# Loading and unpacking the FP4 down weights of a decoder's last feed-forward by another queue and at another stage

## The chip, the cores and the metric

The kernel runs on one core of a Trainium2 chip. A core has five engines, each with its own instruction queue that it works through in order: TensorE (PE, matmuls; PEld is its loading of weights), VectorE (DVE), ScalarE (ACT), GpSimd (POOL) and SyncE (SP, which here only issues transfers). Transfers (DMA) can be issued from SP, ACT or POOL; they run beside the engines, and an instruction that needs the data waits for the landing. The metric is the device time of one execution in microseconds (us).

## The reference

A decoder of two layers with a layer norm after each sublayer, on x of 4 batches x 512 tokens x 512 features, in float32:

```python
x = _layernorm(x + _L0_attn_ref(x, ...))                       # phase A
x = _layernorm(x + _L0_xattn_ref(x, ctx_2048, ctx_2048, ...))  # phase B
x = _layernorm(x + _L0_ffn_ref(x, ...))                        # phase C
x = _layernorm(x + _L1_attn_ref(x, ...))                       # phase D
x = _layernorm(x + _L1_xattn_ref(x, ctx_2048, mask))           # phase E
x = _layernorm(x + _L1_ffn_ref(x, ...))                        # phase F
```

Two phases matter here. E is a cross attention of one head over `ctx` (512 rows of 512) with a mask: scores x·ctx / sqrt(512), softmax, and the readout of the same ctx rows. F is a gated feed-forward with weights packed in FP4, eight codes to a 32-bit word, and one float16 scale for each group of 128 inputs:

```python
w_gu = _dequant_fp4(gate_up_packed, gate_up_scales, 128)   # 2 x 1408 outputs, 512 inputs
w_down = _dequant_fp4(down_packed, down_scales, 128)       # 512 outputs, 1408 inputs
gate, up = split(x @ w_gu.T)
y = (silu(gate) * up) @ w_down.T
return y / sqrt(mean(y * y) + 1e-6)
```

## The kernel before

**Arithmetic.** Tiles are 128 partitions x 512. Where float32 accuracy is wanted, a value is held as a pair of float32r tiles, a rounded high part and the remainder. `split` (L135) makes the pair: the high part by a copy on ACT (L144, "CAST" in the profile), the low part as source minus high part by a tensor_tensor (L147), on DVE or, if asked for, on POOL. `split` also notes the last low part that was given to POOL in `self.low[True]`. A product of two pairs is three matmuls (L155 to L157).

**Order of the work.** Each phase is a Python generator for one batch: A0 to A3, B0, and so on to F3. `lanes` (L1307) steps two of them in turn, so that the end of one batch lies beside the start of the next; background generators prepare weights. `BESIDE` (L40) lists them as (first, last, key): such a generator makes one step per round while the last task started is one from `first` to `last`. `("E2", "E2", "F")` says: step `l1_ffn_weights` from the start of E2 to the start of E3. `need(key, ready)` (L1300) steps a generator on the spot until `ready()` holds. Within a generator, `Pipe.later(n, f)` calls `f` after n calls of `tick`. From the instructions that come of this, a scheduler of the tile framework makes the final order on each engine, and gives out buffers from pools of fixed size (69 "o", 13 "t", 12 "x", 4 "w" buffers in SBUF; 8 banks of PSUM). `issue_after(ins)` keeps an instruction behind `ins` in that order.

**Cross attention (E, `l1_xattn`, L1068).** For each batch: load x and the mask (mk); load ctx transposed (tiles ecT) and make pairs (ecTh on ACT, ecTl on POOL); transpose x on PE (ex) and make pairs (exh on ACT, exl on DVE); load ctx (ecn) and make pairs (ecnh on ACT, ecnl on POOL); scores es on PE; minimum and mask on DVE (ee, L1094); exponential on ACT (L1095); transpose (ep) and make pairs; readout pv on PE; add to x on DVE (L427); statistics (L212, L213); normalize (L236); store by SP (L239). All its loads go by SP's queue.

**Feed-forward (F, `l1_ffn`, L1172).** For each of 11 groups i of 128 inner features, the gate (u = 0) and up (u = 1) products each take four PSUM tiles fg (L1238), which are scaled and summed by ACT (L1186, L1190), DVE (L1194) and POOL (L1198); then silu on ACT (L1202), the product on DVE (L1206), a pair (L1211 on ACT, L1212 on POOL), and the down product facc on PE (L1221) with the pair `self.dn[i]`.

**F's weights.** `l1_ffn_codes` (L1108, key "F0", beside D) turns the gate and up codes into float values and stores them in a scratch in HBM, gu_codes. `l1_ffn_weights` (L1145, key "F") then loads, for each i, the two gate/up tiles from that scratch, the down scales (p4s) and the packed down codes (tile "p4" of the "w" pool, `p<-in_dn_p` in the profile), all by SP; `F_LOAD` = 5 ticks later, `down` unpacks: a shift and a mask on DVE (L1127, L1128), a multiplication by the scales on DVE (L1154), a high part on ACT (L144) and a low part on POOL (L147). The same operations are run eleven times, once for each i. L1232 makes F0 pull that generator until `self.dn` holds the next i.

In the profiled execution, two of the bit operations of each of the first four down loads stand in D, at 1056.9 to 1065.6 us; the multiplications and pairs start at 1156.2 (first multiplication) and 1202.3 (first high part), and end at 1318.4 (last low part), in F0.

Of the kernel before, what the change touches and what calls it, by code (L numbers as in the profile page):

```python
# [12 lines left out]
F16 = mybir.dt.float16  # L13
BF16 = mybir.dt.bfloat16
I32 = mybir.dt.int32
# [6 lines left out]
B, S, D = 4, 512, 512  # L22
P = 128
# [8 lines left out]
LOG_EXP = "natural_log_exp_and_others"  # L32
D_NEXT = 7
B_NEXT = 13
F_LOAD = 5
CODES_EVERY = 3
F_SCALED, F_ACT, F_PAIR, F_DOWN = 1, 5, 3, 9
ORDER = "A0 A1 A2 A3 B0 B1 B2 B3 C0 C1 C2 C3 D0 D1 D2 D3 E0 E1 E2 E3 F0 F1 F2 F3"

BESIDE = [("A1", "A3", "C0"), ("A3", "B0", ("B", 0)), ("B0", "B2", "C"), ("C3", "D0", "D"), ("D1", "D3", "F0"), ("E2", "E2", "F")]  # L40


class Pipe:
# [25 lines left out]
class Net:  # L69
# [1076 lines left out]
    def l1_ffn_weights(self):  # L1146

        yield from self.bg["F0"]
        nc, a, bits = self.nc, self.a, self.bits
        pipe = Pipe()  # L1150

        def down(w, sc):
            f = bits(w)
            nc.vector.scalar_tensor_tensor(f, f, 2.0 ** 126, sc, ALU.mult, ALU.mult)  # L1154
            self.dn.append(self.split(f, "p4", lo_eng=nc.gpsimd))

        for i in range(11):
            for u in range(2):
                pipe.tick()
                self.gu[i, u] = self.o("gu", F32R)  # L1160
                self.load(self.gu[i, u].bitcast(F32), self.gu_codes[i * 2 + u])
                yield
            pipe.tick()
            sc = self.load(self.t("p4s", F16), a["dn_s"][i : i + 1, :].to_broadcast([P, 512]))
            pipe.later(F_LOAD, down, self.load(self.w("p4", I32), a["dn_p"][i]), sc)
            yield
        yield from pipe.drain()

    def l1_ffn(self, b):
        nc = self.nc  # L1170
        pipe = Pipe()
# [57 lines left out]
            acc[t] = f  # L1229

        for i in range(11):
            self.need("F", lambda: len(self.dn) > min(10, i + 1))  # L1232
            for u in range(2):
                for g in range(4):
                    pipe.tick()
                    ps = self.pa("fg")
                    for n in range(2):
                        nc.tensor.matmul(ps, self.gu[i, u][:, g * P : (g + 1) * P], xT[g][n], start=n == 0, stop=n == 1)  # L1238
                    pipe.later(F_SCALED, scaled, i, u, g, ps)
                    yield  # L1240
# [93 lines left out]
def body(tc, args, phases=range(6)):  # L1334
    with ExitStack() as ctx:
# [9 lines left out]
        def step(n):  # L1345
            if len(phases) == 6:
                for first, last, key in BESIDE:
                    if plain.index(first) < n <= plain.index(last) + 1:
# [74 lines left out]
```

## Time and profile before

| what | value |
|---|---|
| median of 3 runs | 1580.09 us (1579.72 to 1582.03) |
| the profiled execution | 1580.57 us |
| its span, first to last instruction | 1578.9 us |
| granted TensorE clock | 0.994 |
| instructions | 25669 |
| gate and up products of F1 and F2 start at | 1338.2 and 1412.0 us |
| 128x512 matmul, start to start, in full flow | 0.2268 us |
| multiplication by the scales, L1154 (min / median / max of 11) | 658 / 689 / 1640 ns |
| shift L1127, mask L1128 (medians of all 33) | 542, 485 ns |
| high part of a p4 tile on ACT (median of 11) | 620 ns |
| low part of a p4 tile on POOL (median of 11) | 1292 ns |

How to read it: a group of instructions is named by its line, engine and operation, then output<-inputs, the tile forms and the count; busy time is the time in which an engine ran instructions. In a timeline, a line begins with its start and its length in us, and joins neighbours of one kind (x4); "[7.39 <-ACT exh L144]" at its end says that the engine had been idle for 7.39 us and that the end of ACT's exh released it. In the list of transfers, the last two columns are KB of one and the median us from issue to landing. Matmuls overlap in the pipeline, so a single one shows 0.39 us while one starts each 0.2268.

### The profile page before, as it was taken

The numbers are of one execution on the slowest core, as the hardware profiler recorded it, in microseconds if no ns is written. First come the engines' busy times: TensorE is split into PE (matmuls) and PEld (weight loads), VectorE is DVE, ScalarE is ACT, GpSimd is POOL, SyncE is SP. The second block draws the span as 40 slices with busy tenths as digits, with TensorE's granted clock in tenths as the row PEclk, the third lists the DMA queues.
The fourth block names the chain that finished last, engine by engine and source line by source line (L and its number), as shares of the span: only waits on it lengthen the run. The fifth ranks groups of instructions, "written<-read, shape, count | busy, mean of one in ns | idle before, by whom it ended". The sixth has DMA issues, their size and how long they took to land.

```text
span 1578.9 us, 25669 instructions
## 1 busy us (share of the span) xinstructions
PE 1512.4 (96%) x8222; PEld 1090.9 (69%) x8222; DVE 1214.0 (77%) x2594; ACT 1041.7 (66%) x2240; POOL 687.8 (44%) x704
## 2 busy tenths in 40 slices
PE   8999998999999999999999999999999999999996
PEld 6888775555544764477777668777687677787885
DVE  6486688898876678777577797767886898888896
ACT  5334667888778877887696864969634445545554
POOL 6665783656535303430435323353324344344342
PEclk9999999999999999999999999999999999999998
DMA  7044874444224534753434345633336630020101
GB/s 256 29 160 140 266 235 151 156 165 139 71 74 126 189 132 131 208 180 130 134 101 120 103 140 148 173 96 91 130 119 220 233 113 12 20 81 1 54 1 54
DMA packets 138759, 200.72 MB, mean 127 GB/s; under 512 B 17776, under 2 KB 52592, under 8 KB 138624
## 3 DMA queue, kind: packets, MB, share of 16 engines
q1 hardware_dynamic: 127584, 178.03, 35.5%
q10 hardware_dynamic: 6912, 12.59, 2.8%
q0 software_dynamic: 4128, 8.46, 2.2%
q8 instruction: 65, 1.06, 0.3%
q14 instruction: 70, 0.57, 0.1%
HBM read 121.94 MB, written 51.90 MB: 110 GB/s over the span
## 4 chain that ended last, share of the span: by engine, by line
PE 50%; DVE 11%; ACT 9%; issue 6%; DMA 3%; POOL 2%; SPq 0%; ACTq 0%; DVEq 0%; POOLq 0%
PE fg L1238 7%; PE facc L1221 5%; DVE fg L1194 3%; PE dT L986 3%; PE dn L794 2%; PE bo L500 2%; PE pg L740 2%; ACT de L976 2%; PE pu L742 2%; PE do L1006 2%; PE bT L249 2%; PE had L808 2%; PE bs L528 2%; PE ds L961 2%; PE dq L155 1%
## 5 line engine op out<-in xcount | busy, mean ns | idle before, releaser
L1194 DVE SCALAR_TENSOR_TENSOR fg<-fg,gs,fg 128x512 f32<-128x512 f32 x220 | 163.1, 745 | 30.4 <-ACT fg L1186 15.6
L976 ACT ACTIVATE de<-de,dm 128x128 f32<-128x128 f32 (+3 forms) x256 | 142.8, 562 | 11.5 <-DVE dm L972 11.3
L1238 PE MATMUL fg<-fxh,gu 128*128 128x512 f32 x352 | 140.4, 399 | 6.2 <-DVE fg L1194 3.1
L972 DVE CUSTOM_DVE_ANT_0 de<-ds,negm,thr 128x128 f32<-128x128 f32 (+3 forms) x256 | 126.3, 546 | 18.4 <-PE ds L961 15.8
L1238 PE MATMUL fg<-fxl,gu 128*128 128x512 f32 x352 | 137.5, 391 | 0.1
L717 POOL TENSOR_TENSOR hl<-g,hh 128x512 fp32r<-128x512 f32 x64 | 83.2, 1307 | 110.8 <-ACT hh L716 90.7
L484 POOL TENSOR_SCALAR be<-be,bsm 128x512 f32<-128x512 f32 x128 | 93.4, 742 | 85.3 <-DVE bsm L482 53.7
L1198 POOL TENSOR_TENSOR fg<-fg,fg 128x512 f32<-128x512 f32 x44 | 60.1, 1367 | 140.3 <-DVE fg L1194 56.7
L478 ACT ACTIVATE be<-bs,bsm 128x512 f32<-128x512 f32 x128 | 87.3, 689 | 32.4 <-DVE bsm L476 31.0
L898 POOL TENSOR_TENSOR dql<-dqf,dqh 128x512 fp32r<-128x512 f32 x32 | 41.4, 1295 | 150.6 <-ACT dqh L897 150.5
L986 PE MATMUL dT<-ident,de 128*128 128x128 f32 x640 | 91.3, 278 | 8.4 <-ACT de L976 6.4
L986 PEld LDWEIGHTS dT<-ident,de 128*128 128x128 f32 x640 | 71.7, 141 | 27.5 <-ACT de L976 14.8
L1238 PEld LDWEIGHTS fg<-fxh,gu 128*128 128x128 f32 x352 | 66.0, 188 | 30.6 <-DVE fg L1194 13.5
L476 DVE TENSOR_REDUCE bsm<-bs 128x1 f32<-128x512 f32 x128 | 83.0, 674 | 2.3 <-PE bs L528 2.3
L249 PEld LDWEIGHTS bT<-ident,be 128*128 128x128 f32 x512 | 54.9, 141 | 29.5 <-issue 15.6
L1238 PEld LDWEIGHTS fg<-fxl,gu 128*128 128x128 f32 x352 | 66.2, 188 | 12.8 <-DVE fxl L147 0.4
L1186 ACT ACTIVATE fg<-fg,gs 128x512 f32<-128x512 f32 x88 | 60.1, 683 | 20.6 <-PE fg L1238 20.6
L249 PE MATMUL bT<-ident,be 128*128 128x128 f32 x512 | 71.2, 280 | 1.4 <-POOL be L484 0.9
L500 PE MATMUL bo<-bpT,cT 128*64 128x512 f32 x256 | 71.4, 618 | 1.0 <-ACT bpT L491 1.0
L1212 POOL TENSOR_TENSOR fhl<-fg,fhh 128x512 fp32r<-128x512 f32 x44 | 58.5, 1330 | 29.9 <-ACT fhh L1211 29.7
L740 PE MATMUL pg<-qT,tb 128*128 128x512 bf16 x256 | 66.8, 381 | 4.4 <-ACT qT L702 2.8
L1190 ACT ACTIVATE fg<-fg,gs 128x512 f32<-128x512 f32 x44 | 30.3, 689 | 60.5 <-PE fg L1238 60.4
(357 smaller groups left out, 4685.3 us busy)
## 6 DMA issues: line engine op xcount, KB each, us to landing
x<-x SPq DMA_DIRECT2D x176, 256.0 KB, 3.2
had_scratch<-hw SPq DMA_DIRECT2D x64, 256.0 KB, 2.3
z<-had_scratch SPq DMA_DIRECT2D x64, 256.0 KB, 5.9
stk<-dqh SPq DMA_DIRECT2D x192, 64.0 KB, 2.1
tw<-in_wd_t SPq DMA_DIRECT2D x32, 256.0 KB, 4.0
p<-in_gu_p SPq DMA_DIRECT2D x22, 256.0 KB, 3.1
gu_codes<-gu SPq DMA_DIRECT2D x22, 256.0 KB, 3.1
gu<-gu_codes SPq DMA_DIRECT2D x22, 256.0 KB, 4.6
```

Of the source, the lines that this page charges most:

```text
L249: self.nc.tensor.transpose(pt[:, i * P : (i + 1) * P], srcs[i][:, j * P : (j + 1) * P], self.ident)
L476: nc.vector.tensor_reduce(sm[:, h : h + 1], ps, AX.X, ALU.max, negate=True)
L478: nc.scalar.activation(e, ps, AF.Exp, bias=sm[:, h : h + 1], accum_out=sm[:, 2 + h : 3 + h])
L484: nc.gpsimd.tensor_scalar(es[h][i], es[h][i], sm[:, 4 + h : 5 + h], 1.0, ALU.mult, ALU.mult)
L500: nc.tensor.matmul(po[0][h * 64 : h * 64 + 64, :], cT[j][:, c : c + 64], pTs[h], start=j == 0, stop=j == NT - 1)
L717: nc.gpsimd.tensor_tensor(lo, g, hi.bitcast(F32), ALU.subtract)
L740: nc.tensor.matmul(pg, tern["wg_t"][k, c][:, m], qT[k], start=k == 0, stop=k == NT - 1)
L972: nc.vector.tensor_tensor_reduce(es[i], ps, self.negm[:, 384 - P * i :], -1.0, self.thr[:, i : i + 1], ALU.add, ALU.min, n4[:, i : i + 1])
L976: nc.scalar.activation(es[i], es[i], AF.Exp, bias=n4[:, i : i + 1], scale=-1.0, accum_out=den[:, hh * 4 + i : hh * 4 + i + 1])
L986: nc.tensor.transpose(pt[:, o + (i - j) * P : o + (i - j + 1) * P], es[i][:, j * P : (j + 1) * P], self.ident)
L1194: self.emitted["DVE"] = nc.vector.scalar_tensor_tensor(y[u], ps, s, y[u], ALU.mult, ALU.add)
L1238: nc.tensor.matmul(ps, self.gu[i, u][:, g * P : (g + 1) * P], xT[g][n], start=n == 0, stop=n == 1)
```

## The change

The eleven loads of packed down codes are issued by POOL's queue instead of SP's, each kept behind the POOL low part that was emitted last. They and the unpacking come first in `l1_ffn_weights`, four ticks between load and unpacking, with two steps per tile; the 22 gate/up loads follow when all eleven are unpacked. The generator is stepped from the start of E1 to the start of F0. F0 now waits for the gate/up loads instead of the length of `self.dn`. The operations of `down` are the same.

```diff
-F_LOAD = 5
...
-BESIDE = [("A1", "A3", "C0"), ..., ("D1", "D3", "F0"), ("E2", "E2", "F")]
+BESIDE = [("A1", "A3", "C0"), ..., ("D1", "D3", "F0"), ("E1", "E3", "F")]
...
         for i in range(11):
+            pipe.tick()
+
+            w = self.w("p4", I32)
+            with self.tc.issue_after(self.low[True].ins):
+                nc.gpsimd.dma_start(w, a["dn_p"][i])
+            pipe.later(4, down, w, self.load(self.t("p4s", F16), a["dn_s"][i : i + 1, :].to_broadcast([P, 512])))
+            yield
+            pipe.tick()
+            yield
+        yield from pipe.drain()
+        for i in range(11):
             for u in range(2):
-                pipe.tick()
                 self.gu[i, u] = self.o("gu", F32R)
                 self.load(self.gu[i, u].bitcast(F32), self.gu_codes[i * 2 + u])
                 yield
-            pipe.tick()
-            sc = self.load(self.t("p4s", F16), a["dn_s"][i : i + 1, :].to_broadcast([P, 512]))
-            pipe.later(F_LOAD, down, self.load(self.w("p4", I32), a["dn_p"][i]), sc)
-            yield
-        yield from pipe.drain()
...
-            self.need("F", lambda: len(self.dn) > min(10, i + 1))
+            self.need("F", lambda: (min(10, i + 1), 1) in self.gu)
```

Lines of the changed kernel are those of before less one up to the weights' loop, and plus four behind it.

More of the change, by code (lines that the diff above doesn't have):

```diff
@@ L38 @@
 ORDER = "A0 A1 A2 A3 B0 B1 B2 B3 C0 C1 C2 C3 D0 D1 D2 D3 E0 E1 E2 E3 F0 F1 F2 F3"
-BESIDE = [("A1", "A3", "C0"), ("A3", "B0", ("B", 0)), ("B0", "B2", "C"), ("C3", "D0", "D"), ("D1", "D3", "F0"), ("E2", "E2", "F")]
+BESIDE = [("A1", "A3", "C0"), ("A3", "B0", ("B", 0)), ("B0", "B2", "C"), ("C3", "D0", "D"), ("D1", "D3", "F0"), ("E1", "E3", "F")]
 class Pipe:
```

## The prediction

> **What bounds the kernel now.** I read the engine totals first, then the chain that ended last.
>
> ```profile
> PE 1512.4 (96%) x8222; PEld 1090.9 (69%) x8222; DVE 1214.0 (77%) x2594; ACT 1041.7 (66%) x2240; POOL 687.8 (44%) x704
> PE 50%; DVE 11%; ACT 9%; issue 6%; DMA 3%; POOL 2%; SPq 0%; ACTq 0%; DVEq 0%; POOLq 0%
> ```
>
> TensorE (PE) is busy 96% of 1578.9 us, so a change can win only where PE has holes and lose wherever it makes one. I therefore asked for the busy time of each engine in stretches around the change: E1 to E2, and the three 74-us stretches in which F0, F1 and F2 do the same work. The columns are the stretch, its length, then PE, PEld, DVE, ACT and POOL (instructions in brackets), the granted clock, the DMA share and GB/s.
>
> ```profile
> 1180.00:1206.00 26.00, 22.86 (x116) 17.87 (x114) 16.19 (x34) 16.73 (x36) 15.01 (x12) 1.00 0.79 282
> 1264.00:1338.00 74.00, 70.76 (x302) 55.12 (x301) 65.53 (x100) 35.70 (x58) 33.42 (x26) 1.00 0.19 63
> 1338.00:1412.00 74.00, 73.22 (x327) 58.89 (x326) 64.38 (x112) 40.42 (x72) 29.49 (x22) 1.00 0.13 40
> 1412.00:1486.00 74.00, 73.28 (x328) 58.97 (x327) 64.38 (x111) 40.46 (x72) 29.52 (x22) 1.00 0.14 43
> ```
>
> See that F0 gets 302 matmuls into the time in which F1 and F2 do 327 and 328: 25 x 0.2268 us (start to start of the 128x512 matmuls) = 5.7 us lost. And in E1 to E2 PE already has 3.1 us of holes while POOL is busy only 58%. The change moves work from the first kind of stretch to the second.
>
> **What F0 gains.** DVE is the fullest engine beside PE in F0 (65.5 of 74). Of the unpacking there, the groups of instructions in 1286 to 1322 show (busy us, mean ns of one):
>
> ```profile
> L1154 DVE SCALAR_TENSOR_TENSOR p<-p,p4s 128x512 f32<-128x512 f32 x5 | 6.1, 1215 | 0.0
> L1194 DVE SCALAR_TENSOR_TENSOR fg<-fg,gs,fg 128x512 f32<-128x512 f32 x27 | 19.7, 743 | 1.4 <-issue 0.6
> ```
>
> Five scale multiplications take 6.1 us, 1215 ns each, against a median of 689 ns over all eleven; four bit operations add 1.7 us. All of it goes. How much of PE's loss goes with it: by ten-us slices of PE's timeline (gaps beyond the matmuls' own cadence) F0 loses 0.8 and 0.7 from 1270 to 1290, where E3's last operations still stand on DVE, and 1.4, 2.1 and 1.0 from 1290 to 1300 and 1310 to 1330, where the unpacking stands: 4.5. A part of the 1.4 can be the tail's; I take **-4.2**, with -5.7 (the whole loss) and -2 (half of the 4.2, if `fg` is late for other reasons) as ends.
>
> **What goes elsewhere.** Before, four of the loads are unpacked early, in D: eight bit operations, 4.1 us of DVE between 1056.9 and 1065.6, where PE is busy 10.00 and 9.98 of each 10 us. Gain 0; cover: PE is the bound there. SP loses eleven issues and POOL gains eleven. SP's do not stand on the chain: 0. But the order of SP's queue changes too: E1's four ctx row loads (ecn) all stand behind E0's stores (before, two of them ahead), and E3's four behind E2's.
>
> **What E1 and E2 pay.** The count is unchanged: three DVE operations, one ACT rounding, one POOL low part for each of eleven tiles. New is where they stand. The built instruction order says: load k on POOL stands behind the low part of load k-2; and DVE, which works strictly in order, has the three operations of loads 3, 4 and 5 between E1's last exl and E1's ee, and the two bit operations of load 6 between that and the first exl of E2. Each first operation waits for its load to land. So DVE's attention work waits for a loop POOL - DMA - DVE - ACT - POOL. The rows for it:
>
> ```profile
> 1186.70 1.91 DVE L236 TENSOR_SCALAR x<-x,ln 128x512 f32<-128x512 f32 x4
> 1197.84 0.69 DVE L147 TENSOR_TENSOR exl<-ex,exh 128x512 fp32r<-128x512 f32 x1 [7.39 <-ACT exh L144]
> ```
> ```profile
> 1180.90 2.54 POOL L147 TENSOR_TENSOR ecTl<-ecT,ecTh 128x512 fp32r<-128x512 f32 x2 [7.30 <-DVE ln L212]
> 1204.85 5.24 POOL L147 TENSOR_TENSOR ecnl<-ecn,ecnh 128x512 fp32r<-128x512 f32 x4 [0.50 <-DMA ecn<-in_ctx]
> ```
> ```profile
> 1187.27 1.79 SPq L239 DMA_DIRECT2D x<-x  x4
> 1189.15 1.20 SPq L253 DMA_DIRECT2D ecn<-in_ctx  x2
> ```
> ```profile
> 1192.38 0.62 ACT L144 CAST ecnh<-ecn 128x512 fp32r<-128x512 f32 x1 [7.83 <-DMA ecn<-in_ctx]
> ```
> ```profile
> 1198.58 0.50 PE L155 MATMUL es<-ecTh,exh 128*128 128x512 f32 x1 [1.59 <-DVE exl L147]
> ```
> ```profile
> stk<-dqh POOLq DMA_DIRECT2D x64, 64.0 KB, 2.3
> had<-in_had POOLq DMA_DIRECT2D x1, 64.0 KB, 2.2
> ecn<-in_ctx SPq DMA_DIRECT2D x16, 256.0 KB, 5.1
> p<-in_dn_p SPq DMA_DIRECT2D x11, 256.0 KB, 3.1
> ```
>
> See the 7.39 us in which DVE waits, ended by exl, and that PE's next group (es) starts right after it: whatever holds that exl holds PE.
>
> The trace has no 256-KB load by POOL. Its issue: the nearest row is had (L586), 0.73 us; the stk issues (L906) took 0.50 to 0.72. I take 0.73. Its landing: below, 2.2 us (64 KB by POOL); above, 5.1 (256 KB by SP in the crowded E stretch). I take 3.3: the same tile by SP, 3.1, and 0.2 for the queue (stk by POOL 2.3, by SP 2.1).
>
> The replay on before's clock. E1's last ecTl ends at 1183.4; then POOL does low 1 (1.29) to 1184.7, issue 3 to 1185.5, low 2 to 1186.8, issue 4 to 1187.5. DVE: norm of E0 to 1188.6, one exl (moved behind it) to 1189.3, load 3's operations 0.54 + 0.49 + 0.69 to 1191.0, load 4's to 1192.7. Load 5: rounding 0.62 to 1191.6, low 3 to 1192.9, issue to 1193.6, landing 1196.9, operations to 1198.6, three ee to 1200.5 (before: 1190.4). Load 6 stands behind E1's four ecnl and low 4 on POOL. The first ecn lands 3.2 us after its issue (1189.15 to 1192.38 above), is rounded by 1193.0; POOL is free at 1193.6, four ecnl end at 1198.8, low 4 at 1200.1, issue 6 at 1200.8, landing 1204.1, two bit operations 1.03 to 1205.2, exl to 1205.8. Before, that exl ended at 1198.53: **+7.3**. Ends: +6.2 with a landing of 2.2; +11 with 5.1 for the ecn and for load 6 (ecn 1194.9, low parts to 1200.7, issue to 1202.7, landing 1207.8, exl 1209.6). A cost below zero is excluded: nothing in the loop gets shorter. From 1198 before has no hole in PE until about 1226 that could take it up.
>
> Loads 7 to 11 stand in the same loop, one low part apart, between E2's and E1's operations. A round trip (issue 0.73, landing 3.3, three operations 1.72, rounding 0.62, low part 1.29) is 7.7 us for two loads, and the work between them fills most of it: **+1.0**, ends 0 and 3 (five waits of 0.6). At the entry to F0, before loses 2.8 us of PE in 1250 to 1260, where ACT, until 1250.69, has waited 6.48 us for E3's last ecn; all four now wait behind the stores: **+0.3**, ends 0 and 2.
>
> [...]
>
> **Sum**: +7.3 + 1.0 + 0.3 - 4.2 = +4.4. The profiled execution (1580.57, span 1578.9, 1.67 around it) becomes 1585.0; the median of the runs shown, 0.48 less, 1584.5.
>
> **Rivals.**
> - *The halves cancel* (within 0.2%, 3.2 us, about what a measurement of this kernel can tell from no change). Loads land in 2.2 (E pays 6.2), the later waits are 0, and F0 gives all of its 5.7: +0.8, 1580.9. For it: POOL's own rows of 2.2 and 2.3. Against: those are a quarter of the bytes.
> - *Faster, by refund.* One mechanism: between 1220 and 1290 PE loses 7.6 us to its own cadence (0.8, 0.6, 1.9, 2.8, 0.8, 0.7 in the ten-us slices that lose), in part for loads (ACT's 6.48 us for E3's ecn). If those loads go out at their old times, the late start of E2 is taken back there: 7.3 + 1.0 - 7.6 = 0.7, and F0's 4.2 to 5.7 stay as gain: about -4, 1576. It decides from the point at which 6.1 us are given back with F0 at 5.7 (7.3 + 1.0 + 0.3 - 5.7 + 3.2). For it: that wait. Against: E3's ecn now stand behind E2's stores, so they come later with E2.
> - *The loop starves E2 as well.* Landings of 5.1 throughout: +11 at load 6, 3 for the rest, 2 at F0, F0 gains 2 to 4: +12 to +14, about 1593. For it: ecT and ecn land in 5.1 here, at a DMA share of 0.79. Against: ecn at 1189 took 3.2.
> - *It does not do what it says*: excluded, the built order has all eleven unpackings ahead of F0.
>
> **Chances.** Forecast (1583.3 to 1590) 0.38; starved 0.18; cancel 0.18; faster 0.26. Slower 0.56, within 0.2% 0.18, faster 0.26. The likeliest is 1584.5. The range must reach into the refund and most of the starved case: 1575 to 1592. The slower cases' own range is 1583.3 to 1594.
>
> **What would show it.** Right: DVE waits ended by the p load (L1126 after) in 1190 to 1210; the first es of E2 about 7 us late against E1's; F0 with some 320 matmuls in its 74 us. Wrong: POOL issues far from 0.73; p landing far from 3.3; the first es of E2 within 2 us of its old place; F0 still at 302, which would say that E3's tail, not the unpacking, costs F0 its time. I would be most wrong if the holes of 1220 to 1290 close by themselves, or if F0 waits for gate and up loads that now go out last.

## The result and the profile after

The changed kernel takes 1600.47 us in the median (1598.68 to 1603.64, 4 runs) against 1580.95 of the kernel before: a ratio of 1.0129, 95% interval [1.011, 1.0147]. It is slower by some 20 us where 4.4 were forecast, and outside the stated range. The profiled execution took 1599.38 us, its span 1597.6.

The engine totals of the page hardly move:

```profile
PE 1514.2 (95%) x8222; PEld 1095.6 (69%) x8222; DVE 1217.6 (76%) x2594; ACT 1041.1 (65%) x2240; POOL 691.9 (43%) x715
```

The same work, spread over 18.7 us more: the time went into holes. The first thing to do is to find in which stage. I take a few marks in TensorE's timeline of each profile: the last group of dq products (D's last batch), the first score product es of E1, E2 and E3, the first transposes fx of F0 and F1, and the end of the span.

| stage, us | before | after | difference |
|---|---|---|---|
| dq of D's last batch to es of E1 | 145.46 | 146.01 | +0.6 |
| es of E1 to es of E2 | 17.83 | 28.91 | +11.1 |
| es of E2 to es of E3 | 38.87 | 47.69 | +8.8 |
| es of E3 to fx of F0 | 12.13 | 12.99 | +0.9 |
| fx of F0 to fx of F1 | 87.33 | 85.74 | -1.6 |
| fx of F1 to the end | 241.99 | 242.28 | +0.3 |
| dq of D's last batch to the end | 543.61 | 563.62 | +20.0 |

So all of the loss is in E1 and E2. VectorE's timeline of the changed kernel there (start, length, operation; in brackets the idle time before it and what ended it):

```profile
1191.78 1.66 DVE L1153 SCALAR_TENSOR_TENSOR p<-p,p4s 128x512 f32<-128x512 f32 x1
1198.60 1.10 DVE L1126 TENSOR_SCALAR p<-p,i 128x512 int32<-128x512 int32 x1 [5.15 <-DMA p<-in_dn_p]
1199.73 1.36 DVE L1127 TENSOR_SCALAR p<-p,i 128x512 int32<-128x512 int32 x1
1201.13 0.69 DVE L1153 SCALAR_TENSOR_TENSOR p<-p,p4s 128x512 f32<-128x512 f32 x1
1201.74 0.68 DVE L1093 CUSTOM_DVE_ANT_0 ee<-es,pen 128x512 f32<-128x512 f32 x1
...
1205.73 1.11 DVE L1126 TENSOR_SCALAR p<-p,i 128x512 int32<-128x512 int32 x1 [2.08 <-DMA p<-in_dn_p]
1206.88 1.37 DVE L1127 TENSOR_SCALAR p<-p,i 128x512 int32<-128x512 int32 x1
1208.17 0.68 DVE L146 TENSOR_TENSOR exl<-ex,exh 128x512 fp32r<-128x512 f32 x1
```

Read it from below: exl, which before started at 1197.84, comes at 1208.17, behind two bit operations that first waited for load 6 and then took 1.11 and 1.37 us, where the medians before are 0.54 and 0.49; ee, at 1188.53 before, comes at 1201.74, behind load 5. GpSimd's timeline shows the loop that I had replayed, in the order that I had replayed:

```profile
1192.84 0.55 POOL L1161 DMA_DIRECT2D p<-in_dn_p  x1
1194.49 4.93 POOL L146 TENSOR_TENSOR ecnl<-ecn,ecnh 128x512 fp32r<-128x512 f32 x4 [1.09 <-PE es L156]
1199.37 1.44 POOL L146 TENSOR_TENSOR p4l<-p,p4h 128x512 fp32r<-128x512 f32 x1
1200.76 0.56 POOL L1161 DMA_DIRECT2D p<-in_dn_p  x1
```

And TensorE (the wait at 1203.33 was 7.62 us, that at 1240.40 stands in E2):

```profile
1203.33 0.47 PE L248 MATMUL ep<-ident,ee 128*128 128x128 f32 x1 [7.62 <-ACT ee L1094]
...
1208.90 0.79 PE L154 MATMUL es<-ecTh,exh 128*128 128x512 f32 x1 [2.41 <-DVE exl L146]
...
1240.40 0.79 PE L156 MATMUL pv<-ecnh,epl 128*128 128x512 f32 x1 [4.70 <-DVE epl L146]
...
1273.61 0.89 PE L248 MATMUL fx<-ident,x 128*128 128x128 f32 x3 [2.88 <-DMA x<-x]
```

A matmul of 128x512 takes 0.39 us in full flow; those at 1208.90 and 1240.40, the first of this size behind the two holes, took 0.79. The windows show a granted clock of 0.50 there (the last three columns are the granted clock, the DMA share and GB/s). First E1's hole, then E2's:

```profile
1198.00:1200.00 2.00, 0.00 (x0) 0.00 (x0) 1.37 (x2) 0.00 (x0) 2.00 (x3) 0.64 1.06 406
1204.00:1206.00 2.00, 2.00 (x11) 1.76 (x10) 0.27 (x1) 2.00 (x5) 0.71 (x1) 0.50 0.33 123
1212.00:1214.00 2.00, 2.00 (x10) 1.62 (x9) 2.00 (x4) 1.76 (x4) 2.00 (x3) 0.95 0.00 0
```
```profile
1238.00:1240.00 2.00, 0.00 (x0) 0.00 (x0) 1.93 (x5) 1.25 (x3) 1.27 (x1) 0.88 0.00 0
1240.00:1242.00 2.00, 1.59 (x4) 1.31 (x5) 2.00 (x6) 0.85 (x3) 0.00 (x0) 0.50 0.00 0
1242.00:1244.00 2.00, 2.00 (x7) 1.52 (x6) 1.93 (x7) 0.04 (x1) 0.00 (x0) 0.50 0.00 0
1244.00:1246.00 2.00, 2.00 (x6) 1.61 (x5) 1.17 (x3) 0.00 (x0) 0.00 (x0) 0.50 0.69 257
1246.00:1248.00 2.00, 2.00 (x9) 1.62 (x9) 0.75 (x1) 0.00 (x0) 0.00 (x0) 0.92 0.96 302
```

In E2 TensorE stands still from 1235.7. If the clock changed in one step each time, the mean of 0.88 puts its fall to 0.50 at about 1239.5 and that of 0.92 its return at about 1246.3, some 6 us after TensorE had work again at 1240.40 (estimates, as all times of the clock below that are worked out from such means): 6 or 7 matmuls in 2 us instead of 9 to 11. In E1 it stands still from 1195.7; by the means of 0.64 and 0.95 the clock was at 0.50 from about 1198.6 to 1212.2, and so still during E2's first products (es, from 1208.90). F0, for its part, gained what was said:

```profile
1282.40:1356.40 74.00, 72.89 (x319) 58.85 (x318) 57.96 (x96) 34.46 (x55) 27.14 (x21) 1.00 0.14 49
```

That is F0's stretch at the same distance from F1 as before's 1264 to 1338: 319 matmuls instead of 302. The 17 more are all of 128x512 (313 instead of 296, counted by their starts; the transposes of 128x128 stay at 4): a gain of 17 x 0.2268 = 3.9 us.

### The profile page after: what moved, and what is told of

It reads as the page before. It is cut to its first block, busy times and chain, and to the rows that moved or that the text cites. A ratio compares the mean times of both kernels' runs of the same rounds, so it can differ in the third digit from the quotient of the medians.

```text
span 1597.6 us, 25699 instructions
## 1 busy us (share of the span) xinstructions
PE 1514.2 (95%) x8222; PEld 1095.6 (69%) x8222; DVE 1217.6 (76%) x2594; ACT 1041.1 (65%) x2240; POOL 691.9 (43%) x715
## 3 DMA queue, kind: packets, MB, share of 16 engines
q8 instruction: 65, 1.06, 0.3%
## 4 chain that ended last, share of the span: by engine, by line
PE 48%; DVE 12%; ACT 8%; issue 5%; DMA 5%; POOL 2%; SPq 0%; ACTq 0%; DVEq 0%; POOLq 0%
PE fg L1242 8%; PE facc L1225 6%; PE dT L985 3%; PE dn L793 2%; ACT de L975 2%; PE bo L499 2%; PE do L1005 2%; DVE fg L1198 2%; PE bT L248 2%; PE had L807 2%; PE pg L739 2%; PE pu L741 2%; PE ds L960 2%; PE dq L154 2%; PE dq L155 2%
## 5 line engine op out<-in xcount | busy, mean ns | idle before, releaser
L248 PEld LDWEIGHTS bT<-ident,be 128*128 128x128 f32 x512 | 54.9, 141 | 29.4 <-issue 14.4
L1242 PEld LDWEIGHTS fg<-fxl,gu 128*128 128x128 f32 x352 | 66.1, 188 | 12.9 <-DVE fxl L146 0.4
```

Of the source, the lines that this page charges most:

```text
L248: self.nc.tensor.transpose(pt[:, i * P : (i + 1) * P], srcs[i][:, j * P : (j + 1) * P], self.ident)
```

## The experiments

In the profiled executions of the kernels below, D's last batch starts anywhere from 1031.6 to 1040.2 us, after a part of the program in which they do the same work (d_unpack and d_slow alone issue loads ahead of that mark; see there). Single executions so differ by some us for reasons that have nothing to do with the edits. Each result is therefore given twice: the ratio of medians to the kernel before, with its interval, and, for one profiled execution, the difference to before from that mark to the end of the span, by stage. E3 and F0 stand in one column, because their border moves.

| kernel | ratio to before, 95% | D's last batch to E1 | E1 and E2 | E3 and F0 | mark to end |
|---|---|---|---|---|---|
| changed | 1.0129 [1.011, 1.0147] | +0.6 | +19.9 | -0.7 | +20.0 |
| e_early | 1.012 [1.0101, 1.014] | +5.7 | +14.9 | -0.9 | +20.0 |
| e_sp | 1.0068 [1.0046, 1.009] | 0.0 | +13.1 | -0.8 | +13.0 |
| e_alias | 1.0033 [1.002, 1.0045] | +2.0 | +4.6 | -1.1 | +5.5 |
| b_alias | 0.9978 [0.9966, 0.9991] | +2.4 | -0.9 | -4.3 | -2.0 |
| e_warm | 1.0086 [1.007, 1.0101] | +0.6 | +16.7 | -4.3 | +12.7 |
| b_beside | 1.0067 [1.0047, 1.0086] | -0.1 | +9.2 | +0.6 | +10.3 |
| b_pool | 1.0036 [1.0026, 1.0047] | +2.3 | +3.1 | +0.4 | +6.1 |
| b_e2e3 | 1.0019 [1.0005, 1.0033] | 0.0 | +1.0 | +2.1 | +2.9 |
| e_alias_ecn | 1.0016 [1.0004, 1.0029] | +0.6 | +2.3 | -2.8 | +0.1 |
| x_ecn | 1.0126 [1.0104, 1.0148] | +0.6 | +19.4 | +0.5 | +20.7 |
| d_unpack | 1.0068 [1.0051, 1.0084] | +12.8 | +0.6 | -3.8 | +9.7 |
| d_slow | 1.0074 [1.0053, 1.0095] | +3.5 | -0.6 | +7.1 | +9.6 |
| b_ecn | 1.0018 [1.0004, 1.0031] | 0.0 | +0.5 | +1.0 | +2.0 |
| b_ecn1 | 0.9994 [0.9981, 1.0006] | 0.0 | -1.9 | -2.1 | -3.0 |

**No wait for a landing (e_early).**

```diff
+        ws = []
+        for i in range(11):
+            ws.append(self.o("p4", I32))
+            nc.gpsimd.dma_start(ws[i], a["dn_p"][i])
+        yield
         for i in range(11):
             pipe.tick()
-            w = self.w("p4", I32)
-            with self.tc.issue_after(self.low[True].ins):
-                nc.gpsimd.dma_start(w, a["dn_p"][i])
-            pipe.later(4, down, w, self.load(...))
+            pipe.later(4, down, ws[i], self.load(...))
```

> The changed kernel, but all eleven packed tiles have buffers of their own (of the large pool), so GpSimd issues the eleven loads together, before layer 1's second cross attention has begun, and no unpacking waits for a landing. Unpacking stays where it is. Theory 'late landings' (VectorE, in order, waits for loads that can only be issued behind low parts, and TensorE falls to half clock in the holes): most of the 19.5 us come back, 1578 to 1586. Rival 'work' (the 33 operations themselves, stretched beside GpSimd's, cost the time wherever the data are): stays at 1593 or above. Rival 'queue' (loads by GpSimd are slow): nothing sure, early issue hides slow loads too.

It took 1599.0 us, no faster than the changed kernel and where the rival "work" had it: the theory "late landings", as the whole cause, fell. All loads are issued by 1165 and no unpacking waits. But now the scheduler finds them ready and puts nine of the eleven tiles' unpacking on VectorE ahead of E1's first ee, which comes at 1209.54, later than in the changed kernel. A part of that block in VectorE's timeline:

```profile
1199.53 1.77 DVE L1153 SCALAR_TENSOR_TENSOR p<-p,p4s 128x512 f32<-128x512 f32 x1
1201.23 1.51 DVE L1127 TENSOR_SCALAR p<-p,i 128x512 int32<-128x512 int32 x1
1202.66 1.51 DVE L1126 TENSOR_SCALAR p<-p,i 128x512 int32<-128x512 int32 x1
1204.09 1.77 DVE L1153 SCALAR_TENSOR_TENSOR p<-p,p4s 128x512 f32<-128x512 f32 x1
1205.78 0.47 DVE L1127 TENSOR_SCALAR p<-p,i 128x512 int32<-128x512 int32 x1
1206.17 0.53 DVE L1126 TENSOR_SCALAR p<-p,i 128x512 int32<-128x512 int32 x1
1206.63 0.68 DVE L1153 SCALAR_TENSOR_TENSOR p<-p,p4s 128x512 f32<-128x512 f32 x1
```

From 1196.6 to 1205.3 GpSimd is working on low parts, and each operation that starts in that time takes 1.5 to 1.8 us; after that 0.47, 0.53 and 0.68. TensorE's clock was at 0.50 from 1184.5 to 1198.1 and from 1208.4 to 1218.6 there, so the holes and the clock are part of this kernel's loss too. Of its 5.7 us ahead of E1, 3.36 are one wait of TensorE's just before es of E1. So the theory had to be put in other words: what costs is that unpacking stands ahead of the attention's operations on VectorE, be it waiting or working. I call that "order on VectorE" below.

**The other queue (e_sp, b_pool).** e_sp is the changed kernel with SyncE's queue, b_pool the kernel before with GpSimd's:

```diff
-            with self.tc.issue_after(self.low[True].ins):
-                nc.gpsimd.dma_start(w, a["dn_p"][i])
+            nc.sync.dma_start(w, a["dn_p"][i])
```
```diff
-            pipe.later(F_LOAD, down, self.load(self.w("p4", I32), a["dn_p"][i]), sc)
+            w = self.w("p4", I32)
+            nc.gpsimd.dma_start(w, a["dn_p"][i])
+            pipe.later(F_LOAD, down, w, sc)
```

> The changed kernel with the eleven loads issued by SyncE instead of GpSimd, at the same place of the program, with no order against low parts. Rival 'queue': back to 1580 to 1587, since only GpSimd's issuing was slow. Theory 'late landings': the loads still wait for one of four buffers and stand in SyncE's queue among the stores and the loads of the attention, so 1592 to 1605; the first operation of a tile still waits for landings of about 5 us.

> The kernel before with only the queue changed: the eleven loads are issued by GpSimd, without an order against low parts, at before's places. Theory 'order on VectorE': within 2 us of before, 1579 to 1582. Rival 'queue': 5 us slower or more, as each load waits for what stands before it on GpSimd.

e_sp is 7 us faster than the changed kernel by the marks (20.0 - 13.0), some 10 by the ratios, and still 13 or 11 slower than before; its median, 1591.72, lies just under the range of "late landings" and above that of "queue". So GpSimd's queue, together with the place behind low parts that e_sp gives up as well, is a third to a half of the loss, not the whole. It is not the landing itself: two of e_sp's loads, issued by SyncE at 1193.02 and 1193.49, landed after 5.0 and 5.2 us, and VectorE waited 6.42 us there. b_pool missed its expectation: I held the queue alone for harmless, and it costs 6.1 (5.7 by the ratio). Part of b_pool's lies in D (+2.3 of it before E1): four loads are issued behind other work of GpSimd's, and VectorE, which has their bit operations next, waits 7.54 us for the first, where before that wait was 1.13. VectorE's and GpSimd's timelines of b_pool:

```profile
1055.23 0.55 DVE L1127 TENSOR_SCALAR p<-p,i 128x512 int32<-128x512 int32 x1 [7.54 <-DMA p<-in_dn_p]
```
```profile
1050.71 0.53 POOL L906 DMA_DIRECT2D stk<-dql  x1
1051.22 0.58 POOL L1166 DMA_DIRECT2D p<-in_dn_p  x1
```

**The stretch alone (b_beside, b_e2e3).** The kernel before with `("E1", "E3", "F")`, and with `("E2", "E3", "F")`, in place of `("E2", "E2", "F")`; nothing else.

> The kernel before with only the stretch widened (the weights' generator is stepped from the second cross attention to the start of the feed-forward); loads stay with SyncE, interleaved gate, up and down as before. Theory 'order on VectorE' (the unpacking operations stand ahead of the attention's operations on VectorE, which has no room there): slower than before by 4 to 12, since more of the unpacking comes in the second and third cross attention. Rival 'queue' (what costs is GpSimd's issuing and its place behind low parts): 1575 to 1580.

> The kernel before with the stretch lengthened at its end only: from the third cross attention to the start of the feed-forward. Theory 'order on VectorE': some of the five unpackings leave the first feed-forward batch (worth at most 3.9 together) and stand beside the fourth cross attention, where VectorE is about as full: within 3 us of before. Rival 'free room': 1576 to 1577.

The stretch alone costs 10.3 us, half of the loss and within the 4 to 12 expected, with SyncE's queue and before's order of loads. VectorE's timeline of b_beside shows the place that I know from the changed kernel, ahead of ee:

```profile
1196.66 1.19 DVE L1127 TENSOR_SCALAR p<-p,i 128x512 int32<-128x512 int32 x1 [7.35 <-DMA p<-in_dn_p]
```

b_e2e3 frees F0 and pays it back in E3 (the sum of both is +2.1): there was no free room in E3 either.

**The unpacking left out (e_alias, b_alias).**

```diff
         def down(w, sc):
+            if self.dn:
+                self.dn.append(self.dn[0])
+                return
             f = bits(w)
```

> The changed kernel with the unpacking of ten of the eleven tiles left out (all use the first pair; the loads stay). This leaves out 30 VectorE operations, 10 roundings and 10 low parts. Theory 'late landings': nothing in layer 1's cross attention waits any more, and the first feed-forward batch has none of the unpacking: 1572 to 1578. Rival 'order' (the new order of SyncE's queue and the gate and up loads that go out last cost the time): stays above 1585.

> The kernel before with the unpacking of ten of the eleven tiles left out (all use the first pair; the loads stay). It prices what the unpacking costs where it stood: my step for the first feed-forward batch says 4.2 us (2 to 5.7), plus up to 1 in the third cross attention: 1574 to 1578. If it stays within 1 us of 1580, the unpacking was free there and nothing could be gained by moving it.

Without the unpacking of ten tiles the changed kernel loses 5.5 us instead of 20.0: 14.5 us, 1.45 a tile, are the unpacking in E, with the holes and the granted clock of 0.50 that go with it in the changed kernel. Before, the same ten tiles cost 4.3 us in E3 and F0 together (2.0 from the mark to the end, 0.22% or 3.5 us by the medians). So that was all there was to gain. I had expected e_alias below 1578; it took 1585.70, where the rival "order" had it. Something else than unpacking costs time too, and more than the 5.5 us seen against before: e_alias and b_alias leave out the same unpacking and differ by 7.5 us (5.5 + 2.0; 8.7 by the ratios).

**What else (e_alias_ecn, x_ecn, b_ecn, b_ecn1).** E1's four ecn loads issued ahead of E0's stores; in b_ecn those of E2 and E3 too:

```diff
         self.load_pairs(pipe, rows("ctx_t"), "ecT", cT)
+        pre = [self.load(self.o("ecn"), ap) for ap in rows("ctx")] if b == 1 else None
...
+        if pre:
+            for n, f in enumerate(pre):
+                pipe.later(3 + n // 2, lambda f=f: cn.append(self.split(f, "ecn", lo_eng=nc.gpsimd)))
+        else:
+            self.load_pairs(pipe, rows("ctx"), "ecn", cn)
```

> The changed kernel with the unpacking of ten of the eleven tiles left out (as in e_alias, 5.3 us above before), and the four ctx row loads of the second cross attention issued ahead of the first one's stores. Theory 'order of SyncE' (what is left of the loss without unpacking comes from those loads standing behind the stores): ScalarE's roundings and exponentials come early again, 2 to 4 us faster than e_alias, 1578 to 1580. Rival 'elsewhere': within 1 us of e_alias.

> The changed kernel with the four ctx row loads of the second cross attention issued ahead of the first one's stores; nothing else. In my replay GpSimd's low parts of those rows stand ahead of the fifth and sixth down loads on the loop. If they bind the loop: 3 to 6 us faster than the changed kernel, 1594 to 1597. If the loop binds itself (landing of the fifth load, unpacking, low part): within 1.5 us of the changed kernel.

> The kernel before with the ctx row loads of the second to fourth cross attention issued ahead of the stores of the batch before each; nothing else. Theory 'order of SyncE': before too pays for loads behind stores (ScalarE waited 7.8 us for one in the second cross attention and 6.5 in the fourth, with exponentials queued behind): 1 to 4 us faster than before, 1576 to 1579. Rival 'hidden': those waits lie beside TensorE's other work, within 1 us of before; the 5 us between e_alias and e_alias_ecn then came with the changed kernel's order alone.

> As b_ecn, for the second cross attention alone. Theory 'order of SyncE': half of what b_ecn gives or less, 0.5 to 2 us faster than before. Rival 'hidden': no difference.

Without unpacking, the edit takes 5.4 us off by the stages, 1.4 of them ahead of E1; by the medians (1.0033 to 1.0016, 0.17%, 2.7 us) the intervals overlap. With unpacking (x_ecn) it changes nothing: there VectorE is held by the loop itself. In the kernel before it gives nothing that can be told: b_ecn is slightly slower where 1 to 4 us of gain were expected, b_ecn1's interval holds 1. So the order of SyncE's queue is a possible source of a part of those 7.5 us in the changed kernel, as argued from one pair of kernels, not shown, and no rule for others. No kernel here is faster than before beyond its interval except b_alias, which leaves work out.

**The clock (e_warm).**

```diff
+        if b == 2:
+            wm = self.pa("wm")
+            for _ in range(16):
+                nc.tensor.matmul(wm, xT[0][0][:, 0:P], cT[0][0], start=True, stop=True)
         yield from self.value_rows(pipe, pT, cn, x, em[:, 8:12], 4, b)
```

> The changed kernel with sixteen matmuls of no use (3.6 us of TensorE at full clock, into a bank that nobody reads) put between the last transposes and the readout of layer 1's third cross attention, where TensorE waited 4.7 us and came back at half the granted clock. Theory 'clock' (a hole costs its length and then some 3 us at half clock): the matmuls lie in the hole, the clock stays at 1.00, and the kernel gets 2 to 3.5 us faster than the changed one, about 1597.5. Rival 'only the hole' (the clock after the hole costs nothing on the path): 1600 to 1601, no change. Rival 'more work': up to 3.6 slower.

E2 became 3.3 us shorter (44.36 for 47.69), although VectorE released the readout no earlier. The windows of e_warm over the same place:

```profile
1240.00:1242.00 2.00, 1.11 (x6) 0.61 (x4) 1.97 (x5) 0.79 (x2) 1.19 (x1) 1.00 0.00 0
1242.00:1244.00 2.00, 1.64 (x6) 1.05 (x7) 2.00 (x6) 0.88 (x3) 0.00 (x0) 1.00 0.00 0
1244.00:1246.00 2.00, 2.00 (x10) 1.63 (x10) 1.93 (x6) 0.00 (x0) 0.00 (x0) 1.00 0.00 0
```

The clock stays at 1.00, 10 matmuls in 2 us where there were 6. (E1's hole was left as it was, so no run prices the clock of 0.50 behind it.) The kernel as a whole gained more than the 2 to 3.5 us expected, 7.3 us from the mark: another 3.6 came in E3 and F0, because with this build F0's fourth x load is issued with the three others at 1250.9 instead of in a later group at 1268.2 (SyncE's timelines), and the 2.88 us wait of fx is gone. That is a side effect of the scheduler's, not of the clock.

**Unpacking in D (d_unpack, d_slow).** A generator of its own for the eleven loads (SyncE) and `down`, two ticks apart, with three steps a tile (in d_slow six, and beside D3 alone):

```diff
-... ("E1", "E3", "F")]
+... ("D3", "E0", "FD"), ("E2", "E2", "F")]
...
+    def l1_ffn_down(self):
+        yield from self.bg["F0"]
...
+            nc.sync.dma_start(w, a["dn_p"][i])
+            pipe.later(2, down, w, self.load(self.t("p4s", F16), a["dn_s"][i : i + 1, :].to_broadcast([P, 512])))
+            for _ in range(3):
+                yield
```

> All eleven down tiles are loaded by SyncE and unpacked in the last batch of layer 1's self attention and the start of the cross attention, in a generator of their own (two ticks from load to unpacking, three steps a tile); gate and up loads stay beside the third cross attention. Theory 'order on VectorE': there TensorE is the bound and VectorE has room (65 to 75% busy), so the stretch pays little, the cross attention loses nothing, and the first feed-forward batch gains its 3.9: 1575 to 1579. Rival 'any place' (an unpacking costs about 1.7 us wherever VectorE is in order): 1585 or more.

> As d_unpack, but six steps a tile, and only in the last batch of the self attention; what is not done by then (about five tiles by the built order) stands in the third cross attention again, none in the feed-forward. Theory 'order on VectorE': between, 1578 to 1583. Rival 'any place': 1585 or more.

The second half of the expectation came true: E1 and E2 lose nothing (+0.6), and E3 with F0 gain 3.8, as much as b_alias gives. The first half did not: D's last batch and E0 pay 12.8. To this come 1.7 us that stand ahead of the mark (from the dq products of the batch before to those of the last, 31.9 instead of 30.2 us; in d_slow 31.9 too), as four loads are issued there already: 14.4 in sum, 1.3 a tile. VectorE is 67 to 95% busy in the twenty-us stretches from 1040 to 1160, but TensorE again waits for operations that come out late behind the unpacking, and the granted clock is 0.50 from 1156 to 1162 (0.74 in the mean of 1145 to 1165):

```profile
1154.45 0.44 PE L248 MATMUL dF<-ident,do 128*128 128x128 f32 x1 [4.37 <-DVE do L1036]
1158.67 0.48 PE L248 MATMUL dF<-ident,do 128*128 128x128 f32 x1 [1.85 <-DVE do L1036]
```

d_slow pays less in D (3.5 and 1.6 ahead of the mark) and then 6.78 us in one wait of F0's for a gate/up load that its order had put last. Both medians, 1591.29 and 1592.84, lie where the rival "any place" had them. "Any place" is nearer to the truth than I was: every place that I tried outside F0 costs more than F0 did.

## Why the prediction was wrong, step by step

The sum said 7.3 + 1.0 + 0.3 - 4.2 = 4.4. By the marks the same terms came to 11.1 + 8.8 + 3.2 - 3.9, with 0.9 elsewhere: 20, but for rounding.

- **F0's gain, -4.2: right.** 3.9 by the matmuls of the 74-us stretch; b_alias says 3.9 to 4.3 for all that could be had. Two of its readings were off: the stretch from 1286 to 1322 has two bit operations, not four (their 1.7 us is right), and the upper end of 5.7 took 25 matmuls for 128x512. By starts, F1 has 12 more of these than F0 and 14 more transposes of 128x128, one of which starts each 0.11 us, so the whole loss was about 4.2.
- **The entry to F0, +0.3 with 2 as an upper end: too small, 3.2.** es of E3 to fx of F0 grew by 0.9, and between the first fx and that stretch the changed kernel loses 2.3 us of F0's gain again (3.9 - 1.6), most of it, as I estimate, in the 2.88 us for F0's last x load and the clock after it (0.91 in the mean of 1272 to 1274, 0.50 from 1274 to 1276, 0.74 from 1276 to 1278).
- **Load 6 ahead of E2's exl, +7.3: the mechanism right, the size 11.1.** The chain of the replay stands in the trace, instruction for instruction. Three of its terms were too small, and they make up the missing 3.8 us. GpSimd was through with the four ecnl at 1199.4; es of E1 stands 0.76 us earlier than before, so on before's clock that is 1.4 later than replayed. The landing took 4.4 us for load 6 (issue ended 1201.3, operation 1205.73), not 3.3: 1.1 more. (Load 5's took 5.2, but VectorE was through with the ee behind it and waited 2.08 us for load 6.) I had a row of 5.1 for this very stretch and preferred one from quiet stages; the DMA share here is 1.01 to 1.06 from 1196 to 1204. The two bit operations: 1.11 and 1.37, not 0.54 and 0.49, another 1.4. The upper end of +11 adds up to about +10.5 by its own terms (four ecnl from 1194.9 end at 1200.1, not 1200.7).
- **Loads 7 to 11, +1.0 with 3 as an upper end: this is the step that failed; 8.8.** I priced five waits and not the work itself. What TensorE lost in E2 stands in its timeline: the one hole of 4.70 us, 3.3 for the clock of 0.50 behind it (by e_warm), and some 1.7 (an estimate: half of the 3.3 us from 1208.90 to 1212.2, as from 1243.6 to 1246.1 a 128x512 matmul starts each 0.43 us instead of 0.2268) for the clock of 0.50 that E1's hole left. That is 9.7, a little more than the 8.8. The hole ends with epl, which VectorE reaches only behind the unpacking: from es of E2 until then 16 unpacking operations took 14.9 us there, 5.8 more than they take alone, and waits for landings 2.1 (1.14 and 1.00). The operations had been counted at their medians, though the prediction's own row showed multiplications at 1215 instead of 689 ns. In the changed kernel the eight bit operations that start while a low part of GpSimd's runs take 1.15 us in the mean, one that starts between two low parts 3.02, the other thirteen 0.50; that is 7.7 us in E1 and E2 together, and 1.9 more for two multiplications (1.66 instead of 0.69). I had used this effect to credit F0 and not to charge E.
- **What no step held: the clock.** A hole of 4.7 us cost 3.3 more, by e_warm, and E1's hole of 7.62 us left the clock at 0.50 for 13.6 us, whose price no run shows. In the kernel before the granted clock is 1.00 in the four stretches that the prediction shows, so no row showed it; my replay made a hole of many us in E1 and put no price on what comes after it. How long a hole has to be for the clock to fall, and what brings it back, no run here settles: the times of the holes seen stand at the end.
- **D, gain 0: right** (+0.6).
- **"No cover after 1198": right.** Nothing was refunded; the rival "faster, by refund" is refuted, E2 lost more in its turn. "The loop starves E2 as well" (+12 to +14) had the right place and was still too mild.
- **GpSimd's issues, priced at 0.73: too much, and the operations beside GpSimd's not priced.** The eleven issues took 0.54 to 0.64 us; before, the stk issues from 1063 to 1101 took 0.50 each where VectorE was 66 to 100% busy (by ten us from 1060 to 1100). Load 5 came late while VectorE stood idle for 5.15 us, and SyncE's loads in the same place of e_sp landed as late (5.0 and 5.2 us). What I should have priced is the time of VectorE's bit operations beside a low part of GpSimd's, 1.15 us in the mean against 0.50. Why they take longer there no run shows; exl at 1208.17, which also started beside a low part of GpSimd's, took 0.68 us (0.69 before).

What stays open: how far E1's loss would shrink if only the landings or only the stretched operations went away (e_early, with no wait for a landing, loses 12.9 there), what the clock of 0.50 behind E1's hole costs, and the cause of the 7.5 us by which the two kernels without unpacking differ.

## What to carry to other kernels

Background work given to an engine that works in order costs what it delays, not what it lasts (here VectorE stood idle for 5.15 us ahead of load 5's first operation, though the es that the next ee reads had ended at 1194.4, and that ee came at 1201.74; the unpacking of ten tiles cost 14.5 us in E and 4.3 in E3 and F0): look up which operation of the path stands behind it, and price its wait for data, its own time beside the neighbour engine as the trace shows it there, and the clock after the hole (here 0.50 for 13.6 and some 6.8 us). A gain is capped by what leaving the work out gives (here 2 to 4 us); measure or bound that first, and a move that can cost more than it should not be made. When a row from the crowded stage and one from a quiet stage disagree, take the crowded one for the crowded stage (here 5.1 us against 3.1; loads 5 and 6 took 5.2 and 4.4).

## What the runs showed of the hardware

- VectorE's 128x512 operations of the unpacking beside a GpSimd tensor_tensor: bit operations 0.50 us alone, 1.15 in the mean of the eight that started beside one, 3.02 for one that started between two; multiplication by scales 0.69 and 1.66 (changed kernel). In e_early 1.51 and 1.77 for six operations in a row.
- TensorE's granted clock in the changed kernel from E1 to F0's entry: 1.00, or 0.50, by estimates from the means of 2-us windows, from 3.8 us after the last matmul until 5.9 us after work resumed (E2), from 2.8 us until 8.9 us, with a second hole of 2.41 between (E1), and from 2.9 us until 3.4 us (F0's entry). Sixteen matmuls of no use in E2's hole made the stage 3.3 us shorter.
- A 256-KB load issued by GpSimd occupies it for 0.54 to 0.64 us and lands in 3.1 us in the median; load 5, amid SyncE's burst of 1187 to 1200, was issued at 1192.84 and used at 1198.60. Two loads of the same size that SyncE issued at 1193.02 and 1193.49 of e_sp landed after 5.0 and 5.2 us.
- Identical work ahead of the mark differed by up to 8.6 us between profiled executions (1031.6 to 1040.2), more than many of the effects here.
